# Cross-attention with sparsemax and a two-branch FFN: last keys' values and a 32-token tile on column tiles, a threshold update with one instruction less, and new numbers for the planner

## The chip, the cores and the metric

The kernel runs on one core of a Trainium2 chip. The metric is the device time of one launch in microseconds (us); of several runs the median is taken. The profile beside it shows one other execution, instruction by instruction. Its engines are PE (matrix products; PEld is its weight load), DVE, ACT and POOL (element-wise work), and SP, which here issues most DMA transfers. TensorE is PE.

## The reference

Eight batches of 100 tokens attend to 722 keys each, with 16 heads of 32 dimensions, and sparsemax in place of softmax. A feed-forward part follows that takes the length of two products.

```python
h = layernorm(x)                                   # x: 8 x 100 x 512
qh, kh, vh = heads(h @ Wq + bq), heads(ctx @ Wk + bk), heads(ctx @ Wv + bv)   # ctx: 8 x 722 x 512
scores = einsum('bhqd,bhkd->bhqk', qh, kh) * 32 ** -0.5
attn = sparsemax(scores)                           # clip(s - tau, 0), tau so that a row sums to 1
x = x + merge(einsum('bhqk,bhkd->bhqd', attn, vh)) @ Wo + bo
h = layernorm(x)
real, imag = h @ cos(theta + theta_noise), h @ sin(phi + phi_noise)
x = x + sqrt(real * real + imag * imag)
```

All products are done in f32.

## The kernel before

**Tiles.** The 800 tokens are cut into seven token tiles, `TILES` (L29): six of 128 tokens and one of 32, the fourth. Norm, queries, output product and FFN go by token tile; attention goes by batch. Keys are computed transposed (`keys`, L627: head dimensions on partitions, 361 keys in a product). Values are computed in `NC` = 6 chunks of `CK` = 121 keys, the last of 117 (`values`, L648): for each chunk four matmuls of 512 columns, one for each 128 of the 512 input dimensions, gathered in one PSUM bank and copied out by ACT (`values_copy`, L660).

**Scores and thresholds.** `fill` (L670) puts scores into a four-bank PSUM tile `psc`, of which there is one. It works on 32 x 32 tiles of the PE array; the four left-over tokens of each batch go through L677 with 128-row contractions on four 32-column tiles. ACT copies a fill to `s_t` (L699, two buffers). DVE takes the eight largest of every piece of some 30 keys (`tops`, L710, 312 MAX8 a batch), thins them (`rests`, `candidates`), forms a first threshold (`first_bound`) and improves it in five update steps, `REACH` (L79). One step is: mask on DVE (`above`, L777), masked values on POOL (`above_values`, L782), count and its reciprocal on DVE (`above_count`, L788 and L789), and `update` (L791) on DVE, which needs both POOL's product and the count. In the first two steps the move is stretched by 1.2 and 1.1: before the sum, L797 computes `past` from the old threshold, and after it two more small instructions (L801, L803) stretch and bound the new one. The last batch does all this in three parts (5, 4 and 4 columns), the other seven in one of 13. POOL then splits the threshold in three bf16 parts (`parts`), PE transposes them (L840) and ACT copies them.

**Weights and outputs.** `weights` (L878) computes the scores again in transposed form, with keys on partitions (L897), on top of minus the threshold (L884), five pairs of head group and key chunk at a time, into `psc` again. ACT takes relu (L909), and `outputs` (L922) multiplies with the values on four 32-column tiles (L931).

**After attention.** `product` (L524) does the output product (512 columns, four matmuls) and later the two FFN products; `residual`, norm, `square`, `square_sum`, `root` and `result` follow. The last token tile has these steps in smaller pieces (`last_steps_of_all`).

**What sets the order.** Nothing is ordered by hand. Each step is a task of a kind with an engine and an assumed cost (`STEPS`, L93). `Plan.order` (L300) places tasks one by one: on each engine it picks the one that can start first, and among those the one with the smallest due time; on PE a task of the same array shape as the one before (`SHAPE`, L165) is preferred by `STAY`. A due time (L292) is the batch number times `PERIOD`, less the assumed cost of everything that depends on the task, plus a number for its kind (`LAG`, L170). `CHANGE` is what a change of shape is assumed to cost. The buffers (`plan = Plan({...})`, L953) limit what may start. The order found is then the order of the instructions on every engine, SP's DMA issues included, and the chip keeps it. A second, plain version of the whole, in a loop behind the flag `again`, runs only where a threshold did not settle.

Of the kernel before, what the change touches and what calls it, by code (L numbers as in the profile page):

```python
# [11 lines left out]
FP = mybir.dt.float32  # L12
# [31 lines left out]
def fills_of(left_first):  # L44
# [55 lines left out]
    "load k": ("SP", 0.7),  # L100
    "stats": ("DVE", 0.85),
    "deviation": ("ACT", 0.25),
    "normed": ("DVE", 0.65),
    "normed T": ("PE", 0.4),
    "normed copy": ("ACT", 0.45),
    "normed 2": ("DVE", 0.65),
    "add bo": ("POOL", 1.2),
# [8 lines left out]
    "fill copy": ("ACT", 0.1, 0.1),  # L116
    "tops": ("DVE", 0.0, 0.0915),
    "rests": ("DVE", 0.05, 0.185),
    "candidates": ("DVE", 0.6, 0.14),
    "first bound": ("DVE", 0.9, 0.143),  # L120
    "above": ("DVE", 0.1, 0.081),
    "above values": ("POOL", 0.1, 0.157),
    "above count": ("DVE", 0.27, 0.088),
    "update": ("DVE", 0.22, 0.088),
    "update far": ("DVE", 0.5, 0.088),
    "losses": ("DVE", 0.35),
    "checks": ("POOL", 0.4),
    "parts": ("POOL", 1.9),
# [2 lines left out]
    "parts copy last": ("ACT", 0.75),  # L131
    "values": ("PE", 3.43),
    "values copy": ("ACT", 0.55),
    "weights": ("PE", 0.05, 0.25),
    "relu ACT": ("ACT", 0.12, 0.168),
    "relu DVE": ("DVE", 0.12, 0.22),
# [2 lines left out]
    "outputs bias": ("ACT", 0.05, 0.28),  # L139
    "output product": ("PE", 3.43),  # L140
    "residual": ("DVE", 0.65),
    "stats 2": ("DVE", 0.85),
    "ffn": ("PE", 3.43),
    "square": ("ACT", 0.57),
# [25 lines left out]
LAG = {  # L170
    "above": 50.0,
    "above count": -110.0,
    "above values": 205.0,
    "add bo": -160.0,
    "bounded": -25.0,
    "candidates": -10.0,
    "checks": 290.0,
    "deviation": -185.0,
    "ffn": 295.0,
    "fill": -220.0,  # L180
    "fill copy": 5.0,
    "fill last": -215.0,
    "first bound": -140.0,
    "half ffn": 125.0,
    "half result": -265.0,
    "half root": 190.0,
    "half square": 195.0,
    "half sum": 145.0,
    "keys": -45.0,
    "keys bias": -105.0,  # L190
    "keys part": -100.0,
    "leftovers": -60.0,
    "load bias": 245.0,
    "load ctx": 250.0,
    "load k": 225.0,
    "load part": 185.0,
    "load w": 220.0,
    "load x": -195.0,
    "load x again": 115.0,
    "losses": 290.0,  # L200
    "normed": 80.0,
    "normed 2": -300.0,
    "normed copy": -300.0,
    "output product": 285.0,
    "outputs": -135.0,
    "outputs bias": -300.0,
    "parts": -75.0,
    "parts T": 90.0,
    "parts copy last": -280.0,
    "product part": 85.0,  # L210
    "queries": -255.0,
    "queries bias": -105.0,
    "relu ACT": -270.0,
    "relu DVE": -60.0,
    "residual": 70.0,
    "rests": -100.0,
    "result": -240.0,
    "root": -25.0,
    "sines": 210.0,
    "square": -60.0,  # L220
    "square sum": 290.0,
    "stats": 145.0,
    "stats 2": 285.0,
    "store": 245.0,
    "tops": 295.0,
    "turned": 45.0,
    "turns": 205.0,
    "update": -290.0,
    "update far": -300.0,
    "values": 110.0,  # L230
    "values copy": -165.0,
    "verdict": -250.0,
    "verdict T": -135.0,
    "verdict most": -185.0,
    "weights": -125.0,
    "weights relu": 40.0,
}


# [13 lines left out]
class Plan:  # L253
# [41 lines left out]

# [52 lines left out]
def xattn_ffn(  # L348
# [163 lines left out]
    def queries_bias(tk, pieces):  # L512

        for st, at, q, n in pieces:
# [6 lines left out]
                ALU.add,  # L521
            )

    def product(tk, name, lhs, w_sb):  # L524
# [56 lines left out]
    def residual(tk):  # L581
        nc.vector.tensor_tensor(tk["x"], tk["py"], tk["x"], ALU.add)

    def square(tk, k):
        tk["sq", k] = rows.tile([P, DM], FP, name="sq", tag="sq", bufs=2)[: tk["n"]]
        nc.scalar.activation(tk["sq", k], tk["pr", k], AF.Square)  # L586

    def square_sum(tk):
        nc.gpsimd.tensor_tensor(tk["sq", 0], tk["sq", 0], tk["sq", 1], ALU.add)  # L589
# [56 lines left out]
        )  # L646

    def values(st, c):  # L648
        n = min(CK, S - c * CK)
        st["pv", c] = pv = ps1.tile([P, DM], FP, name="pm")  # L650
        for k in range(NG):
            nc.tensor.matmul(  # L652
                pv[:n],
                lhsT=st["c"][:, k, c * CK : c * CK + n],
                rhs=wv_sb[:, k, :],
                start=(k == 0),
                stop=(k == NG - 1),
            )

    def values_copy(st, c):  # L660

        if "v" not in st:
            st["v"] = big.tile([P, NC, DM], FP, name="v_t")
        n = min(CK, S - c * CK)
        nc.scalar.copy(st["v"][:n, c, :], st.pop(("pv", c))[:n])  # L665

# [124 lines left out]
    def update(st, lo, hi, reach):  # L791
        n, before = hi - lo, st["t", lo]
        s_t = small.tile([P, NT], FP, name=f"f{lo}")[:, :n]
        t = small.tile([P, NT], FP, name=f"t{lo} {st['b'] % 2}", bufs=3)
        if reach > 1.0:
            past = small.tile([P, NT], FP, name=f"past{lo}")[:, :n]
            nc.vector.tensor_scalar(past, before[:, :n], 1.0 - reach, None, ALU.mult)  # L797
        nc.vector.tensor_reduce(s_t, st["p"][:, lo:hi], AX.X, ALU.add)  # L798
# [216 lines left out]

    def last_steps(tk, outs):

        py = add("output product", lambda: product(tk, "py", "oT", wo_sb), *outs, *w["o"])
        xi = add("load x again", lambda: set_x(tk), tk["normed"])
        bo_in = add("add bo", lambda: add_bo(tk), xi, w["bo"])  # L1020
        rs = add("residual", lambda: residual(tk), py, bo_in)
        hold("pm", py, [rs])
        _, hT2_in, hT2 = norm_steps(tk, rs, " 2")
        prs, sqs = [], []
        for k, w_sb in enumerate((cos_sb, sin_sb)):
            pr = add(
                "ffn",
                lambda k=k, w_sb=w_sb: product(tk, ("pr", k), "hT", w_sb),
                hT2, sines_done[k],
            )  # L1030
            s = add("square", lambda k=k: square(tk, k), pr)
            hold("pm", pr, [s])
            prs.append(pr)
            sqs.append(s)
        hold("hT", hT2_in, prs)
        ss = add("square sum", lambda: square_sum(tk), *sqs)
        rt = add("root", lambda: root(tk), ss)
        at, n = tk["at"], tk["n"]
        rz = add("result", lambda: result(tk, out.rearrange("b q d -> (b q) d")[at : at + n]), rt)
        hold("n_t", sqs[0], [rz])  # L1040
        hold("n_t", sqs[1], [ss])
        hold("x", xi, [rz])
        return py

# [45 lines left out]
    for b in range(B):  # L1090
# [122 lines left out]
        vs = []  # L1213
        vmm = []
        for c in range(NC):
            v = add("values", lambda st=st, c=c: values(st, c), *c_in, *w["v"])
            e = add("values copy", lambda st=st, c=c: values_copy(st, c), v)
            hold("pm", v, [e])
            vmm.append(v)
            vs.append(e)  # L1220
# [135 lines left out]
    with tc.If(flag > 0):  # L1356
        with tc.For_i(0, B) as b:
# [20 lines left out]
            for c in range(NC):  # L1378
                values(st, c)
                values_copy(st, c)  # L1380
            st["top"] = top = small.tile([P, NT], FP, name="top")
            st["t", 0] = t_all = small.tile([P, NT], FP, name="t_all", bufs=1)
            st["th"] = small.tile([P, NC3 + 1, HG], FP, name="th")
# [96 lines left out]
```

## Time and profile before

| | us |
|---|---|
| median of 3 runs | 611.87 (611.27 to 614.71) |
| the profiled execution | 613.43 |
| its span, first to last instruction | 611.7 |
| PE busy | 591.2 (97%), 6513 matmul records |
| DVE busy | 524.1 (86%) |
| ACT busy | 256.7 (42%) |
| POOL busy | 221.5 (36%) |
| first key product on PE | starts at 7.87 |
| first MAX8 on DVE (L710) | starts at 35.79 |
| last PE matmul | ends at 605.4 |

The page's tenths show a full PE from the second of the 40 slices to the last but one, and DVE at nine tenths or more in most slices between the third and the thirty-eighth:

```profile
PE   5999999899999999999999999999999999999985
DVE  3079999999999979998899989999899979999521
PEclk9999999999999999999999999999999999999998
```

The clock granted to PE is full throughout (mean 0.995). The costliest groups of the page are, on PE, the value products L652 (174.3 us) and the key products L630 (152.1 us); on DVE the MAX8s of L710 (231.1 us). DMA matters in the first 34 us, when ctx and the weights come in at 260 to 380 GB/s; afterwards it carries some tens.

How to read it: a busy PE in such a page counts the time in which a matmul is in the array, so consecutive matmuls overlap; what one costs in a row is the distance of starts. "Idle before" is time an engine waited, with what released it.

### The profile page before, as it was taken

The numbers are of one execution on the slowest core, as the hardware profiler recorded it, in microseconds if no ns is written. First come the engines' busy times: TensorE is split into PE (matmuls) and PEld (weight loads), VectorE is DVE, ScalarE is ACT, GpSimd is POOL, SyncE is SP. The second block draws the span as 40 slices with busy tenths as digits, with TensorE's granted clock in tenths as the row PEclk, the third lists the DMA queues.
The fourth block names the chain that finished last, engine by engine and source line by source line (L and its number), as shares of the span: only waits on it lengthen the run. The fifth ranks groups of instructions, "written<-read, shape, count | busy, mean of one in ns | idle before, by whom it ended". The sixth has DMA issues, their size and how long they took to land.

```text
span 611.7 us, 17204 instructions
## 1 busy us (share of the span) xinstructions
PE 591.2 (97%) x6513; PEld 333.7 (55%) x6513; DVE 524.1 (86%) x3203; ACT 256.7 (42%) x358; POOL 221.5 (36%) x293
## 2 busy tenths in 40 slices
PE   5999999899999999999999999999999999999985
PEld 3755434566556565556456644676347533555544
DVE  3079999999999979998899989999899979999521
ACT  1234352347354436342455425452545343444332
POOL 1677687785500251013320560025221350145202
PEclk9999999999999999999999999999999999999998
DMA  8920012002000020002010102000040000000001
GB/s 302 377 81 26 18 46 88 18 20 98 3 2 20 2 97 3 2 2 98 2 54 3 40 2 98 3 2 1 2 134 3 1 23 2 2 2 19 2 2 38
DMA packets 12472, 26.56 MB, mean 43 GB/s; under 512 B 1872, under 2 KB 2128, under 8 KB 12384
## 3 DMA queue, kind: packets, MB, share of 16 engines
q1 hardware_dynamic: 11952, 24.03, 11.7%
q8 instruction: 53, 0.87, 0.6%
q0 software_dynamic: 432, 1.38, 0.6%
q14 instruction: 35, 0.29, 0.2%
HBM read 23.76 MB, written 1.64 MB: 42 GB/s over the span
## 4 chain that ended last, share of the span: by engine, by line
PE 66%; DVE 24%; issue 5%; ACT 2%; POOL 1%; DMA 1%; SPq 0%; POOLq 0%; ACTq 0%; DVEq 0%
PE pm L630 18%; PE pm L652 16%; DVE cand L710 11%; PE pm L527 7%; PE psc L688 5%; PE psc L897 5%; PE pm L931 5%; PE pm L504 3%; DVE m L777 2%; DVE f L798 2%; PE psc L619 2%; DVE n L788 2%; PE psc L884 2%; PE psc L677 1%; DMA wk_sb<-in_L_xattn_Wk 1%
## 5 line engine op out<-in xcount | busy, mean ns | idle before, releaser
L710 DVE MAX8 cand<-s_t 128x8 f32<-128x30 f32 x2496 | 231.1, 174 | 7.0 <-ACT s_t L699 7.0
L782 POOL TENSOR_TENSOR p<-z,m 128x1040 f32<-128x1040 f32 (+2 forms) x50 | 88.6, 1774 | 248.5 <-DVE m L777 246.9
L652 PE MATMUL pm<-wv_sb,c_t 128*121 128x512 f32 (+1 forms) x384 | 174.3, 599 | 0.0
L630 PE MATMUL pm<-c_t,wk_sb 128*128 128x361 f32 x464 | 152.1, 476 | 0.0
L630 PEld LDWEIGHTS pm<-c_t,wk_sb 128*128 128x128 f32 x464 | 85.3, 191 | 52.8 <-issue 7.8
L652 PEld LDWEIGHTS pm<-wv_sb,c_t 128*121 128x121 f32 (+1 forms) x384 | 67.3, 183 | 83.6 <-issue 80.1
L909 ACT ACTIVATE aT<-psc 121x2000 f32<-121x2000 f32 (+1 forms) x39 | 69.3, 1778 | 57.7 <-PE psc L897 57.7
L699 ACT COPY s_t<-psc 128x1924 f32<-128x1924 f32 (+2 forms) x40 | 69.0, 1724 | 45.6 <-PE psc L688 18.9
L665 ACT COPY v_t<-pm 121x512 f32<-121x512 f32 (+1 forms) x48 | 28.1, 585 | 91.1 <-PE pm L652 91.1
L641 ACT ACTIVATE k_t<-pm,bk_sb 128x361 f32<-128x361 f32 x60 | 33.6, 563 | 71.8 <-PE pm L630 71.6
L798 DVE TENSOR_REDUCE f<-p 128x13 f32<-128x1040 f32 (+2 forms) x50 | 50.8, 1015 | 9.9 <-POOL p L782 9.9
L788 DVE TENSOR_REDUCE n<-m 128x13 f32<-128x1040 bf16 (+2 forms) x50 | 50.7, 1014 | 1.1
L931 PEld LDWEIGHTS pm<-aT,v_t 121*32 121x32 f32 (+1 forms) x1536 | 32.8, 109 | 26.9 <-issue 19.4
L897 PE MATMUL psc<-q_t,k_t 32*121 32x100 f32 (+1 forms) x1536 | 46.6, 262 | 0.0
L897 PEld LDWEIGHTS psc<-q_t,k_t 32*121 32x121 f32 (+1 forms) x1536 | 45.7, 180 | 0.2
L688 PE MATMUL psc<-k_t,q_t 32*32 32x481 f32 (+1 forms) x1536 | 44.1, 474 | 1.2 <-ACT s_t L699 1.2
L931 PE MATMUL pm<-aT,v_t 121*32 121x100 f32 (+1 forms) x1536 | 42.0, 251 | 2.5 <-ACT aT L909 1.8
L504 PEld LDWEIGHTS pm<-hT,wq_sb 128*128 128x128 f32 x224 | 28.6, 191 | 8.7 <-issue 6.3
L504 PE MATMUL pm<-hT,wq_sb 128*128 128x128 f32 (+1 forms) x224 | 29.9, 277 | 0.0
L688 PEld LDWEIGHTS psc<-k_t,q_t 32*32 32x32 f32 x1536 | 14.1, 103 | 26.5 <-issue 18.7
L589 POOL TENSOR_TENSOR sq<-sq 128x512 f32<-128x512 f32 (+1 forms) x6 | 7.6, 1268 | 43.2 <-ACT sq L586 43.2
L527 PE MATMUL pm<-cos_sb,hT 128*128 128x512 f32 (+1 forms) x48 | 22.0, 601 | 0.0
(310 smaller groups left out, 578.5 us busy)
## 6 DMA issues: line engine op xcount, KB each, us to landing
c_t<-in_ctx SPq DMA_DIRECT2D x7, 1444.0 KB, 6.2
x_t<-in_x SPq DMA_DIRECT2D x12, 256.0 KB, 2.7
c_t<-in_ctx SPq DMA_DIRECT2D x4, 361.0 KB, 4.7
out<-sq POOLq DMA_DIRECT2D x5, 256.0 KB, 3.1
wk_sb<-in_L_xattn_Wk SPq DMA_DIRECT2D x4, 256.0 KB, 5.4
wq_sb<-in_L_xattn_Wq SPq DMA_DIRECT2D x4, 256.0 KB, 5.6
cos_sb<-in_L_ffn_theta SPq DMA_DIRECT2D x4, 256.0 KB, 5.4
n_t<-in_L_ffn_theta_noise SPq DMA_DIRECT2D x4, 256.0 KB, 4.0
```

Of the source, the lines that this page charges most:

```text
L504: nc.tensor.matmul(tk["pq"][:, g, : tk["n"]], lhsT=wq_sb[:, c, g * P : (g + 1) * P], rhs=tk["hT"][:, c, :], start=(c == 0), stop=(c == NG ...
L527: nc.tensor.matmul(tk[name], lhsT=tk[lhs][:, c, :], rhs=w_sb[:, c, :], start=(c == 0), stop=(c == NG - 1),)
L630: nc.tensor.matmul(pk, lhsT=wk_sb[:, c, g * P : (g + 1) * P], rhs=st["c"][:, c, i * SH : (i + 1) * SH], start=(c == 0), stop=(c == NG - 1),)
L652: nc.tensor.matmul(pv[:n], lhsT=st["c"][:, k, c * CK : c * CK + n], rhs=wv_sb[:, k, :], start=(k == 0), stop=(k == NG - 1),)
L688: nc.tensor.matmul(psc[b * HD : (b + 1) * HD, j, at : at + EDGE[hi] - EDGE[lo]], lhsT=st["q"][r, g, qb * HD : (qb + 1) * HD], rhs=st["k"][ ...
L699: nc.scalar.copy(s_t[:, :, :n], st["psc"][:, :, :n])
L710: nc.vector.max(st["cand"][:, n, k, :], st["s", f][:, j, at + EDGE[k] - first : at + EDGE[k + 1] - first],)
L782: nc.gpsimd.tensor_tensor(st["p"][:, lo:hi], st["z"][:, lo:hi], st["m"][:, lo:hi], ALU.mult)
L798: nc.vector.tensor_reduce(s_t, st["p"][:, lo:hi], AX.X, ALU.add)
L897: nc.tensor.matmul(psc[:m, j, k * Q : (k + 1) * Q], lhsT=st["k"][r, g, lo : lo + m], rhs=st["q"][r, g, :], start=False, stop=(k == len(PAI ...
L909: nc.scalar.activation(st["aT", n][:CK, :, :w], st["psw"][:CK, :, :w], AF.Relu, scale=SCALE)
L931: nc.tensor.matmul(st["po", g][j * HD : (j + 1) * HD, :Q], lhsT=st["v"][:m, c, f : f + HD], rhs=aT[:m, j, k * Q : (k + 1) * Q], start=(c = ...
```

## The change

- `CK` becomes 128. Five chunks have 128 keys and the last has 82. A new step `values_last` computes these 82 as 64 keys on two 64-wide column tiles (256 columns each) and 18 keys on four 32-wide column tiles (128 columns each). Six copies (`values_last_copy`) put the pieces in place instead of one.
- The 32-token tile has its output product and its two FFN products on four column tiles: column group `j` of the result, 128 columns wide, lies on partitions 32j to 32j+31. `small_residual` and `small_root` bring the pieces back with four instructions each; square and sum work on 128 partitions x 128 columns.
- `update` has no `past` instruction any more: the two stretched steps have three small instructions after the sum, and none before it.
- `STEPS` has new costs, `STAY`, `PERIOD` and all of `LAG` have new values, and a due time has a new term for its batch, `SHIFT`.

```diff
-CK = 121
+CK = P
 NC = 6
+CL = S - (NC - 1) * CK
+CA = 64
+CB = CL - CA
...
-SHAPE = {"fill": 1, "fill last": 2, "outputs": 2, "weights": 3}
+SHAPE = {"fill": 1, "fill last": 2, "outputs": 2, "small product": 2, "values last": 2, "weights": 3}
...
-STAY = 240.0
-PERIOD = 106.0
+STAY = 225.0
+
+SHIFT = (-25.0, 45.0, 35.0, 90.0, 40.0, -10.0, 55.0, -25.0)
+PERIOD = 130.0
...
-            t.due = t.batch * PERIOD - t.rank + LAG.get(t.kind, 0.0)
+            t.due = t.batch * PERIOD + SHIFT[t.batch] - t.rank + LAG.get(t.kind, 0.0)
...
+    def small_product(tk, name, lhs, w_sb):
+        tk[name] = ps1.tile([P, DM], FP, name="pm")[:, :P]
+        for c in range(NG):
+            for j in range(HG):
+                nc.tensor.matmul(
+                    tk[name][j * HD : (j + 1) * HD],
+                    lhsT=tk[lhs][:, c, :],
+                    rhs=w_sb[:, c, j * P : (j + 1) * P],
+                    start=(c == 0),
+                    stop=(c == NG - 1),
+                )
...
+    def small_residual(tk):
+        for j in range(HG):
+            x_j = tk["x"][:, j * P : (j + 1) * P]
+            nc.vector.tensor_tensor(x_j, tk["py"][j * HD : (j + 1) * HD], x_j, ALU.add)
...
+    def small_root(tk):
+
+        for j in range(HG):
+            nc.scalar.activation(
+                tk["sq", 1][:HD, j * P : (j + 1) * P], tk["sq", 0][j * HD : (j + 1) * HD, :P], AF.Sqrt
+            )
+        tk["sq", 0] = tk["sq", 1][:HD]
...
+    def values_last(st):
+
+        st["pv", NC - 1] = pv = ps1.tile([P, DM], FP, name="pm")
+        lo = (NC - 1) * CK
+        for m, n, at in ((CA, CA, 0), (CB, HD, DM * CA // P)):
+            w = DM * n // P
+            for k in range(NG):
+                for j in range(P // n):
+                    nc.tensor.matmul(
+                        pv[j * n : j * n + m, at : at + w],
+                        lhsT=st["c"][:, k, lo : lo + m],
+                        rhs=wv_sb[:, k, j * w : (j + 1) * w],
+                        start=(k == 0),
+                        stop=(k == NG - 1),
+                    )
+            lo += m
...
-        if reach > 1.0:
-            past = small.tile([P, NT], FP, name=f"past{lo}")[:, :n]
-            nc.vector.tensor_scalar(past, before[:, :n], 1.0 - reach, None, ALU.mult)
         nc.vector.tensor_reduce(s_t, st["p"][:, lo:hi], AX.X, ALU.add)
         nc.vector.scalar_tensor_tensor(t[:, :n], s_t, -T_SUM, st["n", lo], ALU.add, ALU.mult)
         if reach > 1.0:
-            nc.vector.scalar_tensor_tensor(t[:, :n], t[:, :n], reach, past, ALU.mult, ALU.add)
-
-            nc.vector.tensor_scalar(t[:, :n], t[:, :n], -T_SUM / S, None, ALU.min)
+            nc.vector.scalar_tensor_tensor(
+                t[:, :n], before[:, :n], (1.0 - reach) / reach, t[:, :n], ALU.mult, ALU.add
+            )
+
+            nc.vector.tensor_scalar(t[:, :n], t[:, :n], reach, -T_SUM / S, ALU.mult, ALU.min)
```

Line numbers: MAX8 is L710 before and L791 after, the value products are L652 and L707 (the last 82 keys L723), `small_product` is L551, the POOL product L782 and L863, the sum in `update` L798 and L876.

More of the change, by code (lines that the diff above doesn't have):

```diff
@@ L133 @@
     "values copy": ("ACT", 0.55),
+    "values last": ("PE", 2.7),
+    "values last copy": ("ACT", 2.0),
     "weights": ("PE", 0.05, 0.25),
@@ L141 @@
     "residual": ("DVE", 0.65),
+    "small product": ("PE", 0.95),
+    "small residual": ("DVE", 0.9),
+    "small square": ("ACT", 0.3),
+    "small sum": ("POOL", 0.45),
+    "small root": ("ACT", 1.1),
     "stats 2": ("DVE", 0.85),
@@ new lines @@
+    "above": -240.0,
+    "above count": 100.0,
+    "above values": -300.0,
+    "add bo": 120.0,
+    "bounded": 220.0,
+    "candidates": -165.0,
+    "checks": 100.0,
+    "deviation": -100.0,
+    "ffn": 290.0,
+    "fill": -290.0,
+    "fill copy": 180.0,
+    "fill last": -285.0,
+    "first bound": 125.0,
+    "half ffn": -95.0,
+    "half result": -265.0,
+    "half root": 200.0,
+    "half square": -210.0,
+    "half sum": 205.0,
+    "keys": -60.0,
+    "keys bias": -140.0,
+    "keys part": -115.0,
@@ new lines @@
+    "queries": -300.0,
+    "queries bias": -255.0,
+    "relu ACT": 220.0,
+    "relu DVE": 65.0,
+    "residual": -60.0,
+    "rests": 260.0,
+    "result": -85.0,
+    "root": -180.0,
+    "sines": -225.0,
+    "small product": 55.0,
+    "small residual": 280.0,
+    "small root": 155.0,
+    "small square": -215.0,
+    "small sum": -5.0,
+    "square": -35.0,
+    "square sum": 225.0,
+    "stats": 205.0,
+    "stats 2": -5.0,
+    "store": -80.0,
+    "tops": 170.0,
+    "turned": 150.0,
@@ L237 @@
+    "turns": 225.0,
+    "update": 175.0,
+    "update far": 270.0,
+    "values": 110.0,
+    "values copy": -225.0,
+    "values last": 300.0,
+    "values last copy": 280.0,
+    "verdict": -145.0,
+    "verdict T": 295.0,
+    "verdict most": -85.0,
+    "weights": -85.0,
+    "weights relu": -300.0,
 }
```

168 lines of the change are left out of this document (79 added, 89 removed).

## The prediction

> **What bounds the kernel now.** I read the page's busy shares, then the chain of waits, then the waits of DVE and PE, then the timelines of the start and the end.
>
> ```profile
> PE 591.2 (97%) x6513; PEld 333.7 (55%) x6513; DVE 524.1 (86%) x3203; ACT 256.7 (42%) x358; POOL 221.5 (36%) x293
> PE 66%; DVE 24%; issue 5%; ACT 2%; POOL 1%; DMA 1%; SPq 0%; POOLq 0%; ACTq 0%; DVEq 0%
> ```
>
> PE is busy in 97% of the span. DVE's 86% hides that it is nearly as tight: its first MAX8 starts at 35.79 and its last threshold update ends at 571.8 (timeline), and in those 536 us it is idle for some 15. So two engines bound this kernel, and a saving on PE alone would soon be stopped by DVE. These lines show where they wait for each other, and what DVE waits for inside a batch:
>
> ```profile
> DVE cand L710 <- ACT s_t L699: 7.0, 5, 2.8
> DVE f L798 <- POOL p L782: 9.9, 16, 1.5
> PE pm L840 <- POOL t L833: 2.5, 1, 2.5
> 32.72 1.09 PE L688 MATMUL psc<-k_t,q_t 32*32 32x481 f32 x32
> 35.79 0.38 DVE L710 MAX8 cand<-s_t 128x8 f32<-128x30 f32 x3 [0.81 <-ACT s_t L699]
> 205.12 0.80 DVE L797 TENSOR_SCALAR past<-t0 0_2729 128x13 f32<-128x13 f32 x1
> 216.88 1.24 DVE L798 TENSOR_REDUCE f<-p 128x13 f32<-128x1040 f32 x1 [0.79 <-POOL p L782]
> ```
>
> The first is time DVE loses to late score tiles (PE's fill, then ACT's copy); the last two show that an update step leaves a 0.8 us hole until POOL's product is there, in which `past` now sits.
>
> **Price list for PE.** Each f32 matmul leaves two records (192 `values` matmuls, 384 records). From the chain:
>
> ```profile
> 34.40 3.43 PE pm L652 x8
> 131.53 3.63 PE pm L652 x8
> 180.93 1.39 PE psc L677 x32
> 27.04 2.43 PE pm L630 x8
> 161.35 2.62 PE pm L630 x8
> ```
>
> A four-matmul product of 512 columns takes 3.43 us between full-array neighbours, 3.63 when both neighbours are small-tile work, 3.53 with one: 0.1 us per border. The same holds for keys (2.43, 2.62). L677 is the nearest row to the new forms: 128-row contractions on four 32-column tiles, 181 columns, 32 records in 1.39 us, 43 ns a record. The other is L931, 100 columns, 40 records from 568.33 to 569.32, 25 ns a record.
>
> **PE, part by part.**
> - Products of the 32-token tile (three): 3.43 each now. After: 32 records of 128 columns on four tiles. Between L931 and L677 lie 25 to 43 ns; in proportion to columns 31 ns, so 1.0 us (bounds 0.8 to 1.4). 3 x (3.43 - 1.0) = **-7.3**.
> - Last values: 3.43 now. After: 16 records of 256 columns on two 64-wide tiles, then 32 records of 128 columns on four (1.0). No row has 64-wide tiles. If both halves run together they cost half of the full form, 1.71; scaled with L677 (174 ns for four records of 181 columns, 0.96 ns a column where the full form has 0.84) 1.97; I take 1.84. If they do not overlap, 3.43. Together 2.84 (bounds 2.5 to 4.8): 8 x (3.43 - 2.84) = **-4.7**. The other five chunks grow from 121 to 128 keys; L652's 121- and 117-key forms both take 599 to 600 ns, so nothing. In `weights` the stationary side grows likewise; L897's 121 and 117 forms differ by 3 ns in 262, so I take 0 (at most 6% of 43 us, 2.6).
> - Borders: in the changed order of PE I count 158 borders between full-array and small-tile work, 174 before: **-1.6**.
>
> Sum: -13.6 on PE. [...]
>
> **Start.** SP now issues two `wk` pieces and the first ctx piece ahead of the `x` tiles, so the first key product needs 0.87 MB landed, not 1.38 MB: I take 6.3 us instead of 7.87. The first fill moves further: PE runs four key parts (first 5.4 us as now, then 3 x 3.65), one transpose (0.5) and four query groups (4 x 0.89), 26.7, then waits for DVE's query bias (0.25 + 0.76), and fills at 27.8, not 32.72; two key products and two query groups (6.6 us) that stood ahead are now behind it. `bk` is issued later (26 DMAs ahead, 20 before); at the 0.55 to 0.68 us that SP needs for one it lands about 23, when the fourth key part's first biases want it. The first MAX8 follows a fill by 3.07: **30.9 instead of 35.79, DVE starts 4.9 earlier.** Bounds: 35.79 (the loads arrive late) and 29.
>
> **DVE.** The shorter update drops 20 `past`. Of the 14 wide ones 11 lie in the 0.8 us hole, and without them DVE waits for POOL just as long; the other three and the six narrow ones are 0.11 to 0.38 each: -2.0. Two tiles' statistics are no longer done before the first MAX8 (2 x 0.83 = +1.7), and the small tile's residual comes in four pieces of some 0.26 for one of 0.59 (the 256-column L568 takes 0.42): +0.4. Together 0. What the new order does is more: of the 35 update steps of batches 0 to 6, 21 have nothing but count and reciprocal (and `past`) between mask and sum, so the hole is open; in the new order 15 have. 6 x 0.8 = **-4.8** (bounds 0 and -4.8). The 7.0 us of late fills: PE gets 13.6 us lighter, but 14 of the 35 steps (7 before) now have score tiles of the next batch inside, which must be there earlier. I take half, **-3.5** (bounds 0 and -7).
> Last update: 571.8 - 4.9 - 4.8 - 3.5 = **558.6**; 555 to 562 by the fills, 568 with a late start and no hole closed.
>
> **The end.** Before: L840's last transposes at 574.27, PE's end 605.4, span's end 611.7, so 37.4 with 3.4 of it PE idle. After: parts on POOL 2.3, then on PE, by rows: norm transposes, an output set and a weight set 3.1; a product part and an ffn product 4.5 (the ffn product stood behind the last outputs; it now covers the wait for a relu); weights and outputs 2.6, a wait of 1.3 for the next relu, weights and outputs 2.1; two product parts, the last outputs, 0.4 for their bias and the last part 4.1; the second ffn product 3.5, beside the norm of the last tile (2.75 from 590.17); its transposes and copy 1.4; four half products 6.9: 29.5. After PE's end 6.3 as now. 558.6 + 2.3 + 29.5 + 6.3 = **596.7** by DVE.
> By PE: 611.7 - 13.6 - 1.6 (start) + 1.0 (query bias) = **597.5** with all of today's idle time inside (7.1 us), 594 with half of it.
> The two bounds lie together, and two engines that take turns lose a little to each other: I take a **span of 598**. The profiled execution took 613.43 for a span of 611.7, so 1.7 is added: 599.7 against 613.43. The median of the runs shown, 611.87, lies 1.6 under the profiled one; I forecast **599**.
>
> ACT gets dearer and is covered: six copies (two of 256, four of 128 columns, about 0.38 and 0.27: 1.85) for one of 0.585 per batch, +10 us on an engine busy 42%; if one of them stands ahead of a score copy or relu that PE waits for, the price is 1.3 at that place. The four-piece root (1.1 for 0.63) delays one tile's store, and nothing waits for it. The planner's other numbers only move instructions.
>
> **Rivals.**
> 1. *DVE has the score tiles too late* (slower). With 14 steps wanting tiles of the next batch, a late fill holds up not a tile loop but a threshold chain, and so the weights of that batch; PE then runs dry behind it as at 118 to 120.6 today. For: by sums of rows, the first fill of batches 2, 3, 4 and 5 comes within about 1.5 us of when DVE asks for it. Against: a fill is late by what PE lags, and PE has become the lighter one; today's five such waits are at most 2.8 us long. It decides from 2.7 us lost in each of six batches on top of the forecast; at 4 us: 599 + 24 = **623**.
> 2. *The two 64-wide halves run one after the other*: values last costs 4.4, +1.0 instead of -0.6 a batch, 8 x 1.6 = 12.8: **612**, no change. Against it: L677's and L931's column tiles do run side by side; one after the other, 32 records of 181 columns at the full form's 0.84 ns would be 4.9 us, and L677 takes 1.39. [...]
> 3. *DVE gains nothing*: PE's -13.6 stands, but the loads are late and the holes stay: last update 568, 568 + 2.3 + 29.5 + 6.3 + 1.7 = **608**.
> 4. *The waits go*: no late fills (last update 555) and half of PE's idle: 594 + 1.7, less the 1.6 of the median: **594**.
>
> **How the numbers follow.** Forecast 0.56 (596 to 604), rival 4 0.14, rival 3 0.12, rival 2 0.07, rival 1 0.11. A measurement of this kernel can tell about 0.5%, 3 us, from no change: faster below 608.8, slower above 614.9. Faster 0.56 + 0.14 + 0.12 = 0.82; within 0.07; slower 0.11. The range leaves out rivals 1 and 2 and reaches over rivals 3 and 4: 592 to 609.
>
> **What would show it.** Right: `small_product` about 1.0 us for 32 records, the last values 2.6 to 3.1 per batch, PE's sum some 13 us down, first MAX8 near 31, last update near 559, bare POOL holes in the threshold steps fewer than before, waits of L791 for s_t under 7 us. Wrong: the two 64-wide halves end to end; a first MAX8 at 35; waits of DVE for score tiles over 15 us in total; PE idle in the middle of the span, which today is 4 us between 30 and 570.

## The result, and the profile after

| | before | changed |
|---|---|---|
| median of nine runs, us | 612.76 | 605.38 (604.06 to 613.4) |
| ratio to before | 1 | 0.9895 [0.9859, 0.9932] |
| the profiled execution / its span | 613.43 / 611.7 | 604.06 / 602.3 |
| PE busy / DVE busy, us | 591.2 / 524.1 | 578.9 / 517.6 |

One of the nine runs, the one of 613.4 us, fell in a slower state with a mean clock of 0.977, and the ratio, with its 95% interval, leaves it out. Two later series of the changed kernel, on two chips, gave 604.45 us (0.9849 [0.9822, 0.9875]) and 608.19 us (0.9915 [0.9889, 0.9942]). It is faster by about 1.1% (0.9 to 1.5% in the three series); the forecast, 599.0, was 2.1% below the 611.87 that it started from.

The page of the changed kernel, its busy time, its tenths and its chain:

```profile
PE 578.9 (96%) x6905; PEld 340.3 (57%) x6905; DVE 517.6 (86%) x3186; ACT 265.2 (44%) x401; POOL 220.5 (37%) x293
PE   6999999999899999999999999999999999999885
DVE  2299999998999889999999899988999997999421
PEclk9999999999999999999999999999999999998989
PE 63%; DVE 30%; POOL 2%; ACT 1%; DMA 1%; issue 1%; SPq 0%; ACTq 0%; POOLq 0%; DVEq 0%
```

PE has 12.3 us less to do. The chain leans on DVE more than before (30% for 24%), and two tenths of PE's clock near the end are down: there the granted clock is 0.50 for 3.4 us at a time, at 553.2 and at 577.1. Such a time is called a half-clock stretch below. The waits of DVE and PE (total, times, longest) answer to those of before:

```profile
DVE cand L791 <- ACT s_t L780: 3.2, 3, 2.7
DVE f L876 <- POOL p L863: 12.5, 19, 0.8
PE pm L920 <- POOL t L913: 5.6, 4, 2.5
```

Late fills cost DVE 3.2 us where they cost 7.0; the holes under POOL's product are bare now (12.5). PE waits for thresholds 5.6 us, not 2.5. From PE's timeline (start, duration; in brackets the wait ahead of it), the new forms and the waits:

```profile
27.77 1.10 PE L769 MATMUL psc<-k_t,q_t 32*32 32x481 f32 x32 [0.76 <-DVE q_t L538]
165.46 0.40 PE L920 MATMUL pm<-ident_b,t 128*128 128x128 bf16 x4 [2.55 <-POOL t L913]
189.84 2.95 PE L723 MATMUL pm<-wv_sb,c_t 128*64 128x256 f32 x48
467.13 1.10 PE L551 MATMUL pm<-cos_sb,hT 128*32 128x128 f32 x32
468.03 1.07 PE L551 MATMUL pm<-sin_sb,hT 128*32 128x128 f32 x32
551.58 0.90 PE L1011 MATMUL pm<-aT,v_t 128*32 128x100 f32 x32 [1.47 <-ACT aT L989]
576.29 0.35 PE L964 MATMUL psc<-tT,neg_b 3*128 3x400 bf16 x4 [2.02 <-ACT aT L989]
```

L920 transposes the parts of a batch's threshold, so its wait is one for the threshold; L989 is the relu of the weights. The small product takes 0.90 us from start to start, and the 48 records of the last values 2.76 (the next instruction starts at 192.60). The first fill is where it was forecast, at 27.8. The waits at 165, 551 and 576 us were not in before's trace. From the first fill on PE waited 7.1 us before and waits 11.0 us now (the 0.76 at 27.77 included). DVE's marks are these:

```profile
30.89 9.20 DVE L791 MAX8 cand<-s_t 128x8 f32<-128x30 f32 x100
506.20 1.56 DVE L791 MAX8 cand<-s_t 128x8 f32<-128x30 f32 x16 [2.69 <-ACT s_t L780]
561.36 0.48 DVE L876 TENSOR_REDUCE f<-p 128x4 f32<-128x320 f32 x1
```

The first MAX8 came at 30.9 as forecast. The last update is done at 562.03, not 558.6; its sum, the third line, ends at 561.84, and that end is the mark used below. The middle line shows the way the end is reached: 506.20 is the last time that DVE waits for a score tile, and so for PE. So the span falls into stretches, and in each of the first three one engine does not wait for the other:

- **A**, from the first MAX8 to batch 1's threshold on PE (165.46): DVE's. It does not wait for PE in it. PE arrives early and waits 2.55 us.
- **B**, from there to DVE's restart at 506.20: PE's, which has no wait of 0.3 us or more in it.
- **C**, to the end of the last update's sum (561.84): DVE's.
- **D**, to the start of PE's last product (594.29): PE and ACT in turns, with a wait for a relu.

That is a theory until experiments lengthen and shorten the stretches one by one. Its rivals are that the new forms alone count, or the new order alone.

### The profile page after: what moved, and what is told of

The parts are those of the page before. It is cut to its first block, busy times and chain, and to the rows that moved or that the text cites. A ratio compares the mean times of both kernels' runs of the same rounds, so it can differ in the third digit from the quotient of the medians.

```text
span 602.3 us, 18030 instructions
## 1 busy us (share of the span) xinstructions
PE 578.9 (96%) x6905; PEld 340.3 (57%) x6905; DVE 517.6 (86%) x3186; ACT 265.2 (44%) x401; POOL 220.5 (37%) x293
## 4 chain that ended last, share of the span: by engine, by line
PE 63%; DVE 30%; POOL 2%; ACT 1%; DMA 1%; issue 1%; SPq 0%; ACTq 0%; POOLq 0%; DVEq 0%
PE pm L686 15%; PE pm L707 15%; DVE cand L791 13%; PE pm L583 6%; PE psc L977 5%; PE pm L1011 5%; PE psc L769 4%; PE pm L525 3%; DVE m L858 3%; DVE f L876 3%; PE pm L723 2%; DVE n L869 2%; PE psc L675 2%; PE psc L964 1%; POOL p L863 1%; PE psc L758 1%
## 5 line engine op out<-in xcount | busy, mean ns | idle before, releaser
L791 DVE MAX8 cand<-s_t 128x8 f32<-128x30 f32 x2496 | 231.1, 184 | 3.3 <-ACT s_t L780 3.2
L863 POOL TENSOR_TENSOR p<-z,m 128x1040 f32<-128x1040 f32 (+2 forms) x50 | 88.5, 1771 | 235.5 <-DVE m L858 230.0
L707 PE MATMUL pm<-wv_sb,c_t 128*128 128x512 f32 x320 | 145.0, 600 | 0.0
L707 PEld LDWEIGHTS pm<-wv_sb,c_t 128*128 128x128 f32 x320 | 58.4, 190 | 71.2 <-issue 69.9
L989 ACT ACTIVATE aT<-psc 128x2000 f32<-128x2000 f32 (+1 forms) x39 | 69.3, 1777 | 50.5 <-PE pm L1011 43.4
L876 DVE TENSOR_REDUCE f<-p 128x13 f32<-128x1040 f32 (+2 forms) x50 | 50.6, 1012 | 12.5 <-POOL p L863 12.5
L736 ACT COPY v_t<-pm 128x512 f32<-128x512 f32 x40 | 23.5, 587 | 70.6 <-PE pm L707 70.5
L977 PE MATMUL psc<-q_t,k_t 32*128 32x100 f32 (+1 forms) x1536 | 48.6, 268 | 0.0
L977 PEld LDWEIGHTS psc<-q_t,k_t 32*128 32x128 f32 (+1 forms) x1536 | 47.3, 183 | 0.5
L1011 PE MATMUL pm<-aT,v_t 128*32 128x100 f32 (+1 forms) x1536 | 42.1, 254 | 1.7 <-ACT aT L989 1.7
L1011 PEld LDWEIGHTS pm<-aT,v_t 128*32 128x32 f32 (+1 forms) x1536 | 33.5, 111 | 6.6 <-ACT aT L989 2.1
L645 POOL TENSOR_TENSOR sq<-sq 128x512 f32<-128x512 f32 x5 | 7.4, 1477 | 55.5 <-ACT sq L642 55.5
L769 PEld LDWEIGHTS psc<-k_t,q_t 32*32 32x32 f32 x1536 | 14.0, 103 | 23.5 <-issue 17.4
L723 PE MATMUL pm<-wv_sb,c_t 128*18 128x128 f32 (+1 forms) x384 | 23.5, 311 | 0.0
```

The source lines that it names most:

```text
L707: nc.tensor.matmul(pv, lhsT=st["c"][:, k, c * CK : (c + 1) * CK], rhs=wv_sb[:, k, :], start=(k == 0), stop=(k == NG - 1),)
L769: nc.tensor.matmul(psc[b * HD : (b + 1) * HD, j, at : at + EDGE[hi] - EDGE[lo]], lhsT=st["q"][r, g, qb * HD : (qb + 1) * HD], rhs=st["k"][ ...
L791: nc.vector.max(st["cand"][:, n, k, :], st["s", f][:, j, at + EDGE[k] - first : at + EDGE[k + 1] - first],)
L863: nc.gpsimd.tensor_tensor(st["p"][:, lo:hi], st["z"][:, lo:hi], st["m"][:, lo:hi], ALU.mult)
L977: nc.tensor.matmul(psc[:m, j, k * Q : (k + 1) * Q], lhsT=st["k"][r, g, lo : lo + m], rhs=st["q"][r, g, :], start=False, stop=(k == len(PAI ...
L989: nc.scalar.activation(st["aT", n][:CK, :, :w], st["psw"][:CK, :, :w], AF.Relu, scale=SCALE)
```

## The experiments

Ratios are to the kernel before in the same series. This table has the stretches of one profile of each kernel on which the argument rests, in us; the other kernels are told in the text.

| kernel | first MAX8 | A | B | C | D | median | ratio |
|---|---|---|---|---|---|---|---|
| changed | 30.89 | 134.57 | 340.74 | 55.64 | 32.45 | 605.38 | 0.9895 |
| valfull | 30.17 | 134.53 | 344.74 | 55.62 | 32.92 | 610.02 | 0.9953 |
| smallfull | 31.05 | 134.89 | 350.05 | 55.61 | 32.45 | 614.21 | 1.0013 |
| oldforms | 30.80 | 135.63 | 354.04 | 55.73 | 35.09 | 620.55 | 1.0103 |
| early | 30.30 | 132.60 | 340.74 | 55.63 | 35.04 | 603.78 | 0.9840 |
| late | 31.82 | 134.95 | 340.75 | 52.26 | 34.89 | 604.24 | 0.9862 |
| both | 30.54 | 132.49 | 342.43 | 52.29 | 34.86 | 601.98 | 0.9809 |
| afterfill | 32.33 | 135.51 | 340.73 | 55.76 | 31.36 | 605.79 | 0.9863 |
| bothfill | 32.20 | 131.76 | 340.75 | 51.97 | 32.39 | 598.62 | 0.9757 |

**newforms and oldforms: order and forms crossed.** In newforms each new function stands in place of the old one, in before's order; in oldforms the other way round, in the new order.

```diff
+        if c == NC - 1:
+            return values_last(st)
```

> The kernel before with every instruction in the order it had, and with the new forms alone (chunks of 128 keys, last 82 keys' values and the 32-token tile on column tiles, the shorter update). Two engines bind: PE gets some 13 us lighter, but the first MAX8 stays near 35.8 and the holes under POOL's products stay, so DVE's threshold chains hold the rest back: 606 to 610 us, with PE idle grown by 5 us or more. Rival, the forms are everything and the order nothing: 602 to 606, as the changed kernel. Rival, the order is everything: 612, as the kernel before.

> The changed kernel in its own order, with the old forms (82 keys' values as four products of 512 columns, the 32-token tile as full products, the update with `past`). Two engines bind: some 13 us of PE work return, of which the waits of PE (11 us in the changed kernel) take up 4 to 6: 611 to 615. Rival, the forms are everything: 612 to 618, all 13 back. Rival, the order is everything: 605 to 607, as the changed kernel.

Measured: newforms 612.70, 0.9982 [0.9963, 1.0]; oldforms 620.55, 1.0103 [1.0072, 1.0134]. By itself newforms looks like the rival in which the order is everything (612), but oldforms has the new order and is slower than before; and the forms cannot be everything when they do next to nothing in newforms. So both rivals fall, and both expectations were too mild. In the old order the forms are worth 0.2%, at the edge of the interval; in the new order 2.1%. The new order alone is 1% slower. In newforms, from the timelines of PE and DVE (the third line is before's):

```profile
500.07 0.40 PE L920 MATMUL pm<-ident_b,t 128*128 128x128 bf16 x4 [3.82 <-POOL t L913]
571.12 0.49 DVE L876 TENSOR_REDUCE f<-p 128x4 f32<-128x320 f32 x1 [0.24 <-POOL p L863]
571.09 0.48 DVE L798 TENSOR_REDUCE f<-p 128x4 f32<-128x320 f32 x1 [0.23 <-POOL p L782]
```

The last sum ends at 571.61, where it ended before. PE's busy time fell by 10.2 us and its waits rose by 9.6 (13.9 to 23.5): DVE holds this order. Its waits price the shorter update:

```profile
DVE f L876 <- POOL p L863: 18.2, 27, 1.5
```

DVE's busy time from 35 to 572 us fell by 7.0, and these holes grew from 9.9 to 18.2.

**valfull and smallfull: one form at a time in full.**

```diff
-        for m, n, at in ((CA, CA, 0), (CB, HD, DM * CA // P)):
...
+        for k in range(NG):
+            nc.tensor.matmul(
+                pv[:CL],
+                lhsT=st["c"][:, k, lo : lo + CL],
+                rhs=wv_sb[:, k, :],
...
-        tk[name] = ps1.tile([P, DM], FP, name="pm")[:, :P]
...
+        product(tk, name, lhs, w_sb)
```

> The changed kernel, only the 82 keys' values in the full form (four products of 512 columns, 3.43 instead of 2.76 us, eight times, so 5.4 us more on PE). If PE binds through the middle of the span: 609 to 611, all of it. If PE's waits for thresholds take it up: 605 to 607.

> The changed kernel, only the 32-token tile's three products in the full form (3.43 instead of some 0.85 us each, 7.7 us more on PE, two of the three after 550 us). If PE binds there: 611 to 613. If the waits of PE between 550 and 580 us take up part: 607 to 610. If the two half-clock stretches near 553 and 577 us hang on the waits and these go: below 606.

Measured: 610.02, 0.9953 [0.9935, 0.997], and 614.21, 1.0013 [0.9994, 1.0032]. In the table A and C stay, within 0.4 us, and B alone grows by more: 4.0 us for the five last values that lie in it (two of the eight lie in A, one in C), and 9.3 for the three small products, which start at 414, 467 and 468 in the changed kernel and so all lie in B, not after 550 as the expectation had it (7.6 of work and 1.7 of a half-clock stretch at 167). Together with that stretch they make the 13.3 of oldforms. So PE's amounts were right and on the path, in B. In smallfull DVE waits 5.48 us for a score tile, where the longest such wait was 2.69:

```profile
483.21 2.83 DVE L773 MAX8 cand<-s_t 128x8 f32<-128x30 f32 x30 [5.48 <-ACT s_t L762]
515.99 1.56 DVE L773 MAX8 cand<-s_t 128x8 f32<-128x30 f32 x16 [2.78 <-ACT s_t L762]
```

**past: the old update in the changed kernel.**

```diff
+            past = small.tile([P, NT], FP, name=f"past{lo}")[:, :n]
+            nc.vector.tensor_scalar(past, before[:, :n], 1.0 - reach, None, ALU.mult)
```

> The changed kernel with the old update, 20 `past` instructions more on DVE, ahead of the sum. The prediction's step: most of them lie in the wait for POOL's product, so 0 to 1 us, 605 to 606. Rival, DVE's instruction count binds: 3 us more, 608 to 609.

607.03, 0.9877 [0.9847, 0.9908]: above the 605 to 606 that was expected, and inside the spread of the changed kernel's three series, so the median cannot tell 0 from 3 us. The profile can: A is 135.27 and C 56.07, 0.7 and 0.4 longer than in the changed kernel (again2 has 134.89 and 56.08 without `past`), B is the same, and DVE's waits for POOL's product fall from 12.5 us to 2.8. So `past` lies in those waits and is worth about 1 us at the most, as forecast.

**tail: two relus split between ACT and DVE.**

```diff
+        if st.get("b") == B - 1 and n in (2, 3):
+            relu_half(st, n, True)
+            relu_half(st, n, False)
+            return
```

> The changed kernel; in the last batch the relu of the third and fourth set of weights is split into two halves, one on ACT and one on DVE, as the last set's already is. If the wait of PE for ACT's relu (2.02 us at 576) and the half-clock stretch right behind it (1.35 us more) are on the path: 1.5 to 3 us less, 602.5 to 604. If DVE's or another chain is as late there: no change, 605 to 606.

606.60, 0.9885 [0.986, 0.991]: no gain. DVE's half waits for ACT's half (13.3 us in three places, the last set's included), and PE's wait at 576 is 2.35 instead of 2.02. The half-clock stretch stayed behind it (mean clock of the span 0.993, as in the changed kernel's profile).

**fourafter and fourbefore: batch 1 with four update steps.**

```diff
+        return st["b"] == 1 and st["steps"] > len(REACH)
```

> The changed kernel without the fifth update step of batch 1 (part of the computation left out: one improvement of the threshold in one of eight batches), so that batch 1's threshold is there some 5 us earlier. If PE's wait of 2.55 us at 165 us is for that threshold, the wait goes and what lies behind it comes earlier: 2 to 3.5 us less, 602 to 603.5. If DVE sets the pace throughout: 5 us less, 600. If later waits take it up: no change, 605 to 606.

> The kernel before without the fifth update step of batch 1 (the same part left out). Its PE never waits for that threshold, so if PE sets its pace in the middle: no change, 612 to 613. If DVE sets the pace there too: up to 5 us less, 607 to 609.

604.79, 0.9843 [0.9807, 0.9879], and 613.26, 0.9987 [0.9971, 1.0003]. In the changed kernel PE's wait at 165 goes; A is 132.57, 2.0 shorter for 5 us of DVE, so PE is close behind. In before, where PE does not wait there, nothing happens. The first ratio overlaps the changed kernel's own, so the profile carries this, not the median.

**again, chain, warm, chainwarm: first attempts at the waits.** chain moved tops, `losses`, the statistics and the norm of other tiles out of the chains of batches 0 and 1; warm put matmuls into PE's waits at 551 and 576.

```diff
+        move(tops, update, 1)
+        move(nth("losses", 1, 0), nth("above count", 1, 0), 1)
...
+        move(stats, nth("above count", 1, 1), 1)
...
+        move(normed, dve[dve.index(nth("update", 1, -1)) + 3], 1)
...
+            if k == 0 and (st.get("b"), n) == WARM[0]:
+                fill_wait(st["po", g], 2)
```

> The changed kernel once more, unchanged, beside the next three. 604 to 608 us; runs differ by where PE's half-clock stretches of some 4 us fall, so a second profile should show them partly at other waits than 551 and 576 us.

> The changed kernel with five instructions' worth of DVE work moved out of the threshold chains of batches 0 and 1 (16 MAX8s of the next batch, `losses`, the statistics and the norm of two later token tiles), nothing left out. PE is the bound and waits 1.41 and 2.55 us for these two thresholds: both waits go, 2.5 to 4 us less, 601.5 to 603. If the time comes back in later waits, because DVE bounds the whole: no change, 605 to 606. If the moved work hits the next batch's tops: slower.

> The changed kernel with idle products on PE in the two waits for a relu at 551 and 576 us (8 and 12 matmuls of 300 columns into unused columns, some 1.2 and 1.7 us), nothing left out. If idle time of 1.5 to 2 us is what drops the clock there: the half-clock stretches behind both waits go, 2 to 3.5 us less, 602 to 603.5, and the mean clock rises to 0.998. If the clock drops for another reason: the stretches stay, 605 to 607.

> Both edits together (the DVE work moved, and idle products in the two waits). If PE's waits and the clock are what the forecast missed, they add up: 599 to 601.5 us, the forecast. If one of them does nothing: as the other alone.

again 604.45, 0.9849, with its two half-clock stretches at the same waits, against the expectation. chain 614.84, 1.0028 [1.0007, 1.0049]: slower, and not by the way that the expectation named for that. Its timelines of PE, POOL and ACT:

```profile
173.55 0.61 PE L939 MATMUL pm<-ident_b,t 128*128 128x128 bf16 x4 [8.26 <-POOL t L932]
170.33 1.26 POOL L538 TENSOR_TENSOR x_t<-x_t,bo_sb 128x512 f32<-128x512 f32 x1 [10.77 <-issue]
142.38 0.29 ACT L514 ACTIVATE sd<-mv,estepst 128x1 f32<-128x1 f32 x1 [3.25 <-DVE mv L510]
```

The norm came later, the `x` buffer that it frees with it, and the `add bo` that waits for this buffer stands on POOL ahead of the threshold's parts: a wait of 8.26 for one of 2.55. The deviation on ACT waited for the moved statistics ahead of a relu, and PE waited 2.20 us for that relu at 144. warm gave 606.96, 0.9888 [0.985, 0.9927], chainwarm 620.40, 1.0098 [1.0061, 1.0135], where 599 to 601.5 was expected. These two, against their expectation, leave something out: their result is off by 0.029 (relative error, the same in both). Their matmuls set the start flag, in a PSUM bank in which other columns are still being summed up; the products of zeros further below set none and lose nothing. That the flag does it is the author's guess from this, for no run changes the flag alone. In warm the stretch at 553 was gone (one came at 562.4 instead), and PE waited 2.40 us at 562 for the threshold, 0.77 in the changed kernel: a slow clock ahead of a wait costs little. At 576 the matmuls stood ahead of a result that ACT's relu waits for, and the wait stayed.

**again2, early, late, both: each DVE stretch relieved, with what hangs on it.**

```diff
+        move(nth("losses", 1, 0), nth("above count", 1, 0))
+        move(nth("normed", 4, 0), nth("update", 1, -1))
+        move(nth("add bo", 2, 0), nth("parts", 1, -1))
...
+        move(nth("residual", 6, 0), last)
+        move(nth("losses", 7, 0), nth("normed 2", 6, 0))
...
+        move(nth("square sum", 5, 0), nth("parts", 7, -1))
```

> The changed kernel unchanged, beside the next three: 604 to 606 us.

> The changed kernel with batch 1's threshold chain relieved: its `losses` (three DVE instructions, 2.0 us there) go into the first wait for POOL's product, the norm of a later token tile (2.41 us under POOL's product) goes behind the last update, and the `add bo` that waits for that norm's buffer goes behind the threshold's parts on POOL. Nothing left out. If DVE bounds the first stretch: the update ends some 4 us earlier, PE's wait at 165 us (2.55) goes, and the span falls by 1.5 to 2.5 us, with last update and end. If PE bounds it: no change.

> The changed kernel with batch 7's chain relieved: `losses` (1.06 us) and a residual (0.66) go behind the last update, and POOL's sum and result of a finished token tile, under which two DVE subtractions take 1.25 instead of 0.18 us, go behind the threshold's parts. Nothing left out. If DVE bounds the third stretch: last MAX8 restart to last update 52 instead of 55.6 us, and the end comes 1.5 to 3 us earlier. If PE bounds it there (its output product ends at 559.5, 0.8 us before it needs the threshold): the chain shrinks all the same but the end moves by 0.8 us at most, more only where no half-clock stretch falls at 552.

> Both. If the stretches stand one behind the other, the gains add: 3 to 5 us below the changed kernel, 599.5 to 602, near the forecast. If one of the two is hidden: as the other alone.

early 603.78, 0.984 [0.9827, 0.9854]; late 604.24, 0.9862 [0.9843, 0.9881]; both 601.98, 0.9809 [0.9784, 0.9834]; again2, the changed kernel, 608.19 and 0.9915 beside them, above the 604 to 606 expected (the two half-clock stretches of its profile are 6.8 us long each). The intervals of early, late and both lie below again2's; but again's, from another chip, overlaps all three, so for early and late the stretches of the profiles carry the argument, not the medians. early shortens A by 2.0 and no other stretch: PE's wait at 165 is gone. late shortens C by 3.4, and both does both. In late and both D grows by 2.4: PE, held by a half-clock stretch that starts at 554.5 and 552.4, is now later than the threshold. In early D grows by a half-clock stretch of its own, 10.2 us long, from 558.8. What POOL did to C is seen in the changed kernel (timelines of DVE and POOL)

```profile
531.74 1.26 DVE L818 TENSOR_TENSOR z<-rest,top 128x32 f32<-128x32 f32 x1
538.64 1.25 DVE L818 TENSOR_TENSOR z<-rest,top 128x32 f32<-128x32 f32 x1
531.46 1.49 POOL L645 TENSOR_TENSOR sq<-sq 128x512 f32<-128x512 f32 x1
538.36 1.49 POOL L652 TENSOR_TENSOR sq<-sq,x_t 128x512 f32<-128x512 f32 x1
```

and in late, where POOL's two sums stand elsewhere:

```profile
533.06 0.18 DVE L835 TENSOR_TENSOR z<-rest,top 128x32 f32<-128x32 f32 x1
538.87 0.18 DVE L835 TENSOR_TENSOR z<-rest,top 128x32 f32<-128x32 f32 x1
```

The same subtraction ends with POOL's instruction, or takes 0.18 where POOL's stands elsewhere: that is 2.15 us, in a stretch that became 3.4 us shorter.

**afterfill and bothfill: the two waits filled with products of zeros.**

```diff
+            if k == 0 and (st.get("b"), n) == (B - 2, 4):
+                fill_wait(st["po", g], 6)
...
+                    lhsT=zeros[:, :HD],
+                    rhs=wo_sb[:, 0, :Q],
+                    start=False,
+                    stop=False,
```

> The changed kernel with products of zeros on PE (24 and 36 matmuls of 100 columns, 1.2 and 1.8 us by the 25 ns a record of the outputs) in its waits for a relu at 551 and 576 us; they add nothing to the sums and nothing waits for them. If the idle time drops the clock: no half-clock stretch behind the two waits, mean clock 0.997 or more; the one at 552 lies ahead of a wait for the threshold and gives little, the one at 576 its 1.3 us: 603 to 604.5. If the clock drops for another reason: stretches as before, 604.5 to 608.

> The same products of zeros in the kernel with both chains relieved, in which PE and not the threshold is late after 551 us: both stretches count there, 1.3 to 3.5 us below it, 598.5 to 600.5. If the clock drops for another reason: 601 to 603.

afterfill 605.79, 0.9863 [0.9838, 0.9889]; bothfill 598.62, 0.9757 [0.9734, 0.9781], the fastest kernel of the study. The stretches, with the granted clock as the third figure from the right, behind both waits in the changed kernel

```profile
552.00:557.00 5.00, 5.00 (x71) 3.51 (x60) 4.76 (x15) 2.98 (x8) 1.78 (x3) 0.66 0.01 3
576.00:581.00 5.00, 4.71 (x79) 3.39 (x79) 0.49 (x1) 1.55 (x4) 0.00 (x0) 0.66 0.00 0
```

and at the same work in bothfill:

```profile
549.00:554.00 5.00, 4.70 (x119) 3.40 (x108) 4.80 (x14) 3.81 (x12) 2.68 (x5) 1.00 0.03 7
572.00:577.00 5.00, 4.71 (x99) 2.87 (x100) 0.99 (x1) 1.42 (x4) 0.00 (x0) 1.00 0.02 3
```

The clock stays full to the end of PE's work in the profiles of both kernels. Alone this gains nothing that can be measured, against its expectation of 603 to 604.5: PE then waits 2.52 us for the threshold at 563, D is 1.1 us shorter, and this profile starts 1.4 us later. (Three of afterfill's six runs have a mean clock of 0.993 or 0.994, near the changed kernel's 0.993; that they had half-clock stretches somewhere is an estimate from this.) With C shortened the products give D back its 32.4, and the median falls by another 3 us. One of the six runs of both had a mean clock of 0.998 without any such products, and took 597.71, which also points to the clock. That 598.62 meets the forecast's 599 is chance, for the forecast had none of these edits.

## Why the prediction was right and where it was wrong

- **Prices of the forms: right.** Small product 0.90 (forecast 1.0), last values 2.76 (2.84), side by side; rival 2 is out. PE's busy time fell by 12.3 though the half-clock stretches in it cost 1.9 us more than before's: 14.2 of lighter work (13.6). One price is missing among them: a change between two forms of small tiles, for which the sum of 13.6 has no term, is not free. From L688's last start to L677's first it is 0.29 us, as long as to a key product, where L688's own steps of the same form are 0.13 to 0.19; from L723's 64-wide to its 32-wide tiles it is 0.31 for steps of 0.21. So each such change costs some 0.1 us here; the 2.76 holds one of them, and the sum came out all the same.
- **Start: right in its marks.** Keys at 5.94 (6.3), first fill 27.77 (27.8), first MAX8 30.89 (30.9).
- **Shorter update and covers: right in size.** newforms and past show the update worth nothing; late fills 3.2 (3.5 forecast to be left), holes 12.5 where newforms has 18.2, 5.7 less by the order (4.8). Rival 1 is out, and so is rival 3: the last update is done at 562.03, not 568. One sign was not well chosen: "bare POOL holes fewer than before" did not show, for there are 19 of them and were 16, because `past` no longer sits in them; against newforms' 27 they are fewer. One reading was too low: DVE's windows have 28.1 us of idle time in those 536 us, not some 15; 16.9 of it are the two waits that the prediction lists.
- **Wrong: "with all of today's idle time inside (7.1 us)".** This is the step that failed. PE's 597.5 took the work out and left the waits as they were, at full clock. The new order moved them: 2.55 at 165, 1.47 at 551, 2.02 at 576 are new, and the total is 11.0 us, 3.1 more than the 7.1 and the query bias. PE idle in the middle of the span, a sign of being wrong in the prediction's own list, showed: 7.4 us between 30 and 570 for 4.0. On top, half-clock stretches cost some 3.3 us of PE's work (behind 551, L977 2.29 for 1.2 us and L583 4.49 for 3.6; behind 576, some 1.35 of L1011 and the product parts). Before lost 1.4 to one: its clock was not full throughout, but 0.50 for 3.4 us from 120.5. So the waits (3.1) and the clock (1.9) took 5.0. Against these stand 0.6 of lighter work and 0.2 of the bias; the start gave PE 0.8 less idle time for the forecast 1.6. That makes 5.0, and from 597.5 to 602.3 it is 4.8. oldforms shows it without the forms: the order costs 1%.
- **Wrong with it: the last update, 558.6 by taking 4.9, 4.8 and 3.5 off one unbroken line of DVE.** DVE's line is broken twice, where PE waits for it at 165 and where it waits for PE at 506. The last update comes at B's end plus C, and B is PE's and hangs on PE's wait at 165. C holds two collisions with POOL (2.15 us), `losses` (1.06) and a residual (0.66), none of them in the forecast; in late the sum of the last update ends at 559.78, in both at 557.75.
- **The end: 29.5 from POOL's parts on was short.** From the last update to PE's end it is 34.2 us (596.2 less 562.03) for the forecast 31.8 (2.3 and 29.5), by the wait of 2.02 where 1.3 was taken and the stretch behind it.
- **The median and the profiled run.** Of the 6.4 us between 599 and 605.38, 4.4 are those of the profiled execution (604.06 for 599.7). The other 2.0 are the spread: the forecast reckoned the median 0.7 below the profiled run, and it lay 1.3 above. The mean clock of the nine runs goes with it: 0.993 or 0.994 from 604.06 to 605.38 us, 0.985 at 607.44 and 609.51, 0.977 at 611.79 and 613.4.

What stays open is which part of the order costs its 1% beyond the waits and the clock that are named here, and why the profile of both has one half-clock stretch, at 208 us, with no wait ahead of it.

## What to carry to other kernels

Where two engines hold each other up, find the last wait of each for the other and cut the span there; a saving counts only in the stretch where its engine never waits, and "today's idle time" belongs to an order, not to a kernel. Before moving an instruction, follow the buffer that it frees to the next instruction that wants it, and see what is queued behind that one on its engine. In this kernel short waits of PE cost twice, once as waits (3.1 us more than forecast) and once by the half-clock stretches behind them (1.9 us more than before's), but only where PE was late afterwards.

## What was not expected of the hardware

- **Half clock after waits of 1.5 to 2 us.** Over the twenty profiles PE has 37 waits of 2.0 to 2.8 us; 20 were followed within 2 us by a half-clock stretch of 3.4 us or more, and 17 were not (2.55 at 165 in the changed kernel was not, 1.47 at 551 was). Filled with products, the same two places kept the full clock in the profiles of afterfill and bothfill (mean clock of the span 0.997 and 0.999; 0.993 in the changed kernel's).
- **Half clock goes with where a wait lies on a grid of 3.41 us.** Every half-clock stretch within PE's work lasts 3.41 us or two, three or four times that, and within a profile all of them start on one grid of 3.41 us. With the spans between 30 us and PE's end cut on this grid, all 18 windows at full clock in which PE is busy less than 42% are followed by half clock, 15 of the 29 between 42 and 57.5%, and 1 of the 3229 above (the one from 204 us in both). This is a count over profiles and not an experiment, and it leaves open what decides between 42 and 57.5%. The same wait for batch 1's threshold is cut in two by the grid in the changed kernel (first line, no half clock behind it) and falls into one window in smallfull (second line; the third is the window behind it). The second and third figures are the window's length and PE's busy time, the third from the right is the clock:

```profile
164.11:167.52 3.41, 2.06 (x10) 1.43 (x11) 3.41 (x40) 1.03 (x5) 1.29 (x7) 1.00 0.00 0
163.66:167.07 3.41, 1.13 (x7) 0.87 (x8) 3.41 (x37) 0.68 (x3) 2.04 (x10) 1.00 0.00 0
167.07:170.48 3.41, 3.41 (x7) 1.96 (x6) 3.41 (x39) 2.13 (x5) 0.00 (x0) 0.50 0.00 0
```

- **Some DVE instructions take longer while POOL computes.** L818, two tensor inputs, takes 1.25 for 0.18 us, and ends within 0.05 us of POOL's instruction both times; L501, one tensor input, took 2.41 for 0.55 under POOL's product of 2.16 (156.80 to 159.2). The last batch's reductions of L876 keep their 0.48 with 0.25 to 0.32 us under POOL's product. Why the one is held and the other is not, no run shows.
- **B repeats to a hundredth.** Eleven profiles with the changed kernel's PE work in B have 340.73 to 340.76 us there; both, with its half-clock stretch at 208, has 342.43, and chain and chainwarm, with half clock up to 177, have 342.56 and 342.63; what spreads from run to run lies at the loads (PE starts between 5.5 and 7.5) and in the clock.
